# Two pieces at fixed places, four banks for the last shared products, two groups' sums on ScalarE and GpSimd, and a place for one turn

## The chip, the cores and the metric

The kernel runs on one core of one Trainium2 chip. The metric is the device time of an execution in microseconds (us). TensorE is called PE in the views, VectorE DVE, ScalarE ACT, GpSimd POOL and SyncE SP; SP and ACT issue most transfers, POOL issues those whose addresses come from a tensor.

## The reference

Input x has 32 sequences of 32 tokens of 256 features, all f32. Four residual steps follow each other; the last one is where most of the change lies.

```python
x = x + attn(cond(x, idx, weights))           # per-sequence mixing, layer norm, 16-head causal attention
x = x + ffn(lora_ffn(x, adapters))            # gated feed-forward with adapters (256 -> 1024 -> 256), then a second one
x = x + memory_attn(causal_attn(x, precision))  # 16 heads; then retrieval from four memory banks
x = x + moe(paged_attn(x, block_tables, kv_lens))

def moe(xt):                                   # 1024 tokens, 16 experts, two chosen for each token
    logits = xt @ Wr.T + bias
    probs = softmax(logits)
    val, idx = top_k(probs, 2)
    w = val / (sum(val) + 1e-9)
    y_e = (silu(xt @ Wg[e]) * (xt @ Wu[e])) @ Wd[e]          # for every expert e: 256 -> 128 -> 256
    routed = sum over the two chosen e of w * y_e
    shared = (silu(xt @ sWg) * (xt @ sWu)) @ sWd
    return routed + shared
```

## The kernel before

The tokens are worked in four quarters of 256 (`NQ = 4`) in the first two steps and in layer 1's first attention, and in eight groups of 128 (`NG = 8`) later. A framework records the program and orders the instructions of each engine; `behind(a, b)` fixes by hand that b stands behind a in its engine's queue. Each engine then runs its queue strictly in that order.

**The feed-forward with attention woven in.** `mha` is a generator with a step per `yield`. For each half j of a quarter it makes scores (L444, kb from L437), then the softmax on DVE and ACT: L456, L460, L461, the exponential L462, L464 to L466. It then turns the weights with four transposes into a bank (L470, "the turn"), copies them on ACT (`PT`, L472), multiplies with the values (L477, sixteen small products) and copies the outcome (`AV`, L484). `layer1(q, held=held)` runs this attention for quarter q, and the products that it puts into the dictionary `held` get a place inside the gated products of `feed_forward(q + 1, z, held)`. `gated` makes eight sums per half of its output in pairs (w_g, w_g, bl_g, or w_u, w_u, bl_u for each sum; L196); `sums_` lists their last matmuls in order. `STAND` says behind which of these sums what was held has to stand:

```python
for k, n in STAND.items():
    for x in held.get(k, ()):
        behind(sums_[n - 1], x)
```

ACT makes the feed-forward's tanh (L593), DVE its products (L594, L595). During the second of these rounds POOL fills a mask (`bad`, L818, L819).

**The expert pieces.** After the router each token has two rows, one for each chosen expert. Rows are ordered by expert into 16 blocks of 128 (`NB = 16`), and a block may hold rows of more than one expert, so there are at most `NP = 31` pieces, each one block with one expert. POOL gathers the blocks' rows (`xg`, L1476): nine gathers stand first in its queue, then a product of the shared expert (L1341), then the other gathers. TensorE turns each block (`xT`, L1566 and L1568). For piece j the expert `ex[j]` and the block `j - bx[j]` are read from registers: DVE copies the block into `xs` (L1577), TensorE multiplies it with the expert's gate and up weights out of `ew` (L1580), ACT and DVE make h (L1592, L1593), TensorE turns h (L1595), ACT copies it (`hT`, L1600), TensorE multiplies with the down weights (L1602), and DVE adds the rows that belong to the piece into `yall` (L1612). As soon as a block's last piece is in, POOL writes the block's rows to `ys_d` in DRAM in the tokens' order (L1617).

**The shared expert.** `shared_in` makes its hidden rows for 512 tokens (L1331, L1336, L1341 or L1343), `shared_out` multiplies for four groups of 128 tokens (L1350) and adds into `acc` (L1354). The first half's products stand at piece 2, the second half's after the last piece. They use the pool `y` of two banks.

**The end.** SP and ACT, in turn, read both rows of each token back from `ys_d`, one transfer for each group (`y2`, L1637). DVE multiplies each row by its weight and adds it to `acc` (L1641, two for each group), and SP (even groups) and ACT (odd groups) write the group out (L1644).

Of the kernel before, what the change touches and what calls it, by code (L numbers as in the profile page):

```python
# [18 lines left out]
F32 = mybir.dt.float32  # L19
I32 = mybir.dt.int32  # L20
AF = mybir.ActivationFunctionType
ALU = mybir.AluOpType
AX = mybir.AxisListType

P = 128
B, S, D = 32, 32, 256
# [23 lines left out]
NE = 16  # L50
# [3 lines left out]
NB = 2 * NT // P  # L54
NP = NB + NE - 1
# [73 lines left out]
def tile_layers(ctx: ExitStack, tc: tile.TileContext, i: dict, out: bass.AP):  # L129
    nc = tc.nc  # L130
    v, s, g_, te = nc.vector, nc.scalar, nc.gpsimd, nc.tensor
# [16 lines left out]
    ident = cpool.tile([P, P], F32, name="ident")  # L148
# [80 lines left out]
    turn = [cpool.tile([P, 2, NG, 32], F32, name=f"turn{j}") for j in range(2)]  # L229
# [3 lines left out]
    with (  # L233
# [169 lines left out]
        def mha(zq, w, q_out, k_out, v_out, ch=first_chain, idle=(), held=None):  # L403
# [27 lines left out]
            for j in range(QG):  # L431
                js = slice(j * P, (j + 1) * P)
                ps = ch.score()
                for m in range(2):

                    kb = ch.tile("kb", [P, 4, 8, 32])
                    v.tensor_tensor(  # L437
                        kb,
                        KT[:, m, js].rearrange("p (b k) -> p b k", b=4).unsqueeze(2).broadcast_to([P, 4, 8, 32]),
                        m8.unsqueeze(1).unsqueeze(3).broadcast_to([P, 4, 8, 32]),  # L440
                        ALU.mult,
                    )
                    for b4 in range(4):
                        mm_ = te.matmul(  # L444
                            ps[32 * b4 : 32 * b4 + 32, m * 256 : (m + 1) * 256],
                            lhsT=QT[:, m, j * P + 32 * b4 : j * P + 32 * b4 + 32],
                            rhs=kb[:, b4].rearrange("p h k -> p (h k)"),
                            start=True,
                            stop=True,
                        )  # L450
                        if held is not None:
                            held.setdefault(("scores", j, m), []).append(mm_)
                    if (j, m) in idle:
                        keep_busy(idle[j, m], ch.bank()[:, 0], w["q"][:, 0, :], mm_)
                sm = ch.tile("sm", [P, 16, 32])
                v.tensor_tensor(  # L456
                    sm, ps.rearrange("p (h k) -> p h k", k=32), C("causal").unsqueeze(1).broadcast_to([P, 16, 32]), ALU.add
                )
                mx = sp.tile([P, 16], F32, tag="mx", name="mx")
                v.tensor_reduce(mx, sm, AX.X, ALU.max)  # L460
                v.tensor_tensor(sm, sm, mx.unsqueeze(2).broadcast_to([P, 16, 32]), ALU.subtract)  # L461
                s.activation(sm, sm, AF.Exp)  # L462
                su = sp.tile([P, 16], F32, tag="su", name="su")
                v.tensor_reduce(su, sm, AX.X, ALU.add)  # L464
                v.reciprocal(su, su)
                weighted.append(v.tensor_tensor(sm, sm, su.unsqueeze(2).broadcast_to([P, 16, 32]), ALU.mult))  # L466
                yield
                pt = tr.tile([P, 4, P], F32, tag="tr", name="tr")
                for hg in range(4):
                    te.transpose(pt[:, hg], sm[:, 4 * hg : 4 * hg + 4, :].rearrange("p h k -> p (h k)"), ident)  # L470
                PT = sp.tile([P, 4, P], F32, tag="PT", name="PT")
                s.copy(PT, pt)  # L472
                yield
                av = tr.tile([P, 4, P], F32, tag="tr", name="tr")
                for b4 in range(4):
                    for hg in range(4):
                        te.matmul(  # L477
                            av[64 * (hg % 2) : 64 * (hg % 2) + 64, hg // 2, 32 * b4 : 32 * b4 + 32],
                            lhsT=vblk[:, j, b4, hg, :],
                            rhs=PT[:, hg, 32 * b4 : 32 * b4 + 32],  # L480
                            start=True,
                            stop=True,
                        )
                s.copy(AV[:, :, js], av[:, :2])  # L484
                yield
# [82 lines left out]

        STAND = {("scores", 1, 0): 4, ("scores", 1, 1): 5, "first": 14, "second": 15, "banks": 16}

        def lora(ps, q, name):

# [471 lines left out]
    with tc.tile_pool(name="w1", bufs=1, reuse_waits="tile") as wp:  # L1046
# [269 lines left out]
        with (  # L1316
# [26 lines left out]
                    eng.tensor_tensor(h, h, pair[1], ALU.mult)  # L1343
                return h

            def shared_out(n, h, pool, tag):
                for j in range(4):
                    g = 4 * n + j
                    ps = pool.tile([P, CH], F32, tag=tag, name=tag)
                    down = te.matmul(  # L1350
                        ps[:, :D], lhsT=h[:, j * P : (j + 1) * P], rhs=sd[:, 0, :], start=True, stop=True
                    )
                    behind(loaded[0][-1], down)
                    v.tensor_tensor(acc[:, g, :], acc[:, g, :], ps[:, :D], ALU.add)  # L1354
# [165 lines left out]
            with (  # L1520
# [39 lines left out]
                for j in range(NP):  # L1560
                    if j == 2:
                        shared_out(0, first_h, yp, "y")
                    if j < NB:
# [2 lines left out]
                            turned = te.transpose(pt[:, k * P : (k + 1) * P], xg[j][:, k * P : (k + 1) * P], ident)  # L1566
                            behind(gus[j - 2] if j > 1 else loaded[0][-1], turned)
                        v.tensor_copy(xT[:, j, :], pt[:, :D])  # L1568
                    w = ew[:, bass.ds(ex[j], 1), :].rearrange("p a n -> p (a n)")
                    at_b = nc.s_assert_within(  # L1570
                        j - bx[j],
                        max(0, j - NE + 1),
                        min(j, NB - 1),
                        skip_runtime_bounds_check_because="a piece's number is its block's and its expert's together",
                    )
                    x = sp.tile([P, 1, D], F32, tag="xs", name="xs")
                    v.tensor_copy(x, xT[:, bass.ds(at_b, 1), :])  # L1577
                    pg = gp.tile([P, CH], F32, tag="gu", name="gu")
                    for k in range(2):
                        mm_ = te.matmul(  # L1580
# [19 lines left out]
                    s.copy(hT, ph[:, :P])  # L1600
                    py = yp.tile([P, CH], F32, tag="y", name="y")
                    yd = te.matmul(py[:, :D], lhsT=hT, rhs=w[:, 2 * D :], start=True, stop=True)  # L1602
                    ys_.append((j, at_b, py))
                    if j == 1:
                        places()


                    while j >= 1 and ys_:
                        k, at_k, py = ys_.pop(0)
                        to_k = yall[:, bass.ds(at_k, 1), :].rearrange("p a n -> p (a n)")  # L1610
                        kept_.append(
                            v.scalar_tensor_tensor(to_k, py[:, :D], own[:, k : k + 1], to_k, ALU.mult, ALU.add)  # L1612
                        )
# [8 lines left out]
                            )  # L1622
                        )
                weigh()
                shared_out(1, shared_in(1, gp, "gu", v, yd), yp, "y")
                behind(picked[-1], *put)
                for j, a in enumerate(put):
                    for b in put[:j]:
# [9 lines left out]
                    y2s.append(y24[:, g % 4])  # L1638
                for g, y2 in enumerate(y2s):
                    for k in range(2):  # L1640
                        v.scalar_tensor_tensor(  # L1641
                            acc[:, g, :], y2[:, k, :], w12[:, k, g : g + 1], acc[:, g, :], ALU.mult, ALU.add
                        )
                    (nc.sync, s)[g % 2].dma_start(out[g * P : (g + 1) * P, :], acc[:, g, :])  # L1644
# [73 lines left out]
```

## Time and profile before

| What | us |
|---|---|
| median of 3 runs | 639.51 (638.82 to 641.37) |
| the profiled execution, its own time | 637.68 |
| its span | 635.9 |
| TensorE busy in the span | 576.7 |
| DVE busy | 383.4 |
| ACT busy | 179.3 |
| POOL busy | 184.0 |

The page gives busy times of each engine, the clock that was granted to TensorE in tenths in 40 slices of the span, and the chain of work that ended last, followed back from the end. Times in the other views are counted from the span's start. A line of the timeline has start, duration, engine, line of the kernel, operation, the tiles written and read with their shapes, the count, and in brackets how long the engine was idle before and what ended that. A line of the windows has a stretch, its length, then the busy time and count for PE, PE's weight loads, DVE, ACT and POOL, and last the granted clock, the DMA share and GB/s.

### The profile page before, as it was taken

To read this page: it belongs to the slowest core of one execution; us is meant where nothing else is said; L and a number is where in the kernel's file an instruction comes from. 1 tells how busy PE (TensorE), PEld (TensorE's weight loads), DVE (VectorE), ACT (ScalarE), POOL (GpSimd) and SP (SyncE) were. 2 spreads that over 40 slices of the span, in tenths; PEclk is the share of its full clock that TensorE was granted. 3 is DMA by queue.
4 is the path that set the end of the run, shared out by engine and by line. 5 is a ranking of instruction groups with operands and counts; after the bars stand their busy time and mean duration, and the time that the engine had idled before them with its cause. 6 is when DMAs were issued, how large, how long until landed. Compare 5 with 4: busy or idle time off the path is not lost.

```text
span 635.9 us, 9278 instructions
## 1 busy us (share of the span) xinstructions
PE 576.7 (91%) x3302; PEld 445.7 (70%) x3302; DVE 383.4 (60%) x893; ACT 179.3 (28%) x487; POOL 184.0 (29%) x268
## 2 busy tenths in 40 slices
PE   3889999999999999999999999997688898799992
PEld 1667878687778786788878886785566676466661
DVE  4847685965856939533382128546377775665655
ACT  1312232422312203122041103324365543312220
POOL 5014001434530048960000000005656402360350
PEclk9979999999999999999999999999599988989997
DMA  6963201645441000000000038004212100220126
GB/s 174 344 246 36 57 2 38 168 129 121 116 129 40 1 13 3 1 2 18 0 1 1 0 112 350 2 1 142 77 57 82 52 2 33 73 82 13 42 84 207
DMA packets 29165, 48.47 MB, mean 76 GB/s; under 512 B 7535, under 2 KB 21248, under 8 KB 28288
## 3 DMA queue, kind: packets, MB, share of 16 engines
q1 hardware_dynamic: 19405, 30.23, 14.0%
q0 software_dynamic: 5184, 15.38, 9.4%
q10 hardware_dynamic: 4531, 2.28, 1.3%
q8 instruction: 26, 0.43, 0.3%
q14 instruction: 19, 0.16, 0.1%
HBM read 36.84 MB, written 11.04 MB: 75 GB/s over the span
## 4 chain that ended last, share of the span: by engine, by line
PE 68%; DVE 18%; issue 4%; ACT 4%; DMA 3%; POOL 2%; another core or an unknown queue 1%; SPq 0%; DVEq 0%; ACTq 0%; POOLq 0%
PE ff L196 31%; PE mm L196 10%; PE gu L1580 4%; PE tr L477 3%; PE y L1602 2%; PE sc L1157 2%; DVE kb L437 2%; PE po L1191 2%; DVE vblk L427 2%; PE mm L939 2%; ACT sm L1172 2%; PE sc L444 1%; PE tr L470 1%; POOL xg L1476 1%
## 5 line engine op out<-in xcount | busy, mean ns | idle before, releaser
L1098 POOL DMA_INDIRECT kv<-rows_d,at x40 | 39.1, 977 | 173.2 <-DVE rsm L1012 152.3
L662 POOL COPY rr<-raw 88x256 f32<-88x256 f32 x64 | 30.3, 506 | 93.8 <-PE tr L525 47.4
L594 DVE SCALAR_TENSOR_TENSOR th<-th,ff 128x512 f32<-128x512 f32 x32 | 21.8, 682 | 38.4 <-ACT th L593 38.3
L437 DVE TENSOR_TENSOR kb<-KT,con 128x1024 f32<-128x1024 f32 x28 | 34.1, 1239 | 9.5 <-ACT KT L410 5.0
L1580 PE MATMUL gu<-ew,xs 128*128 x124 | 34.8, 401 | 2.1 <-DVE xs L1577 1.3
L593 ACT ACTIVATE th<-ff 128x512 f32<-128x512 f32 x32 | 19.1, 597 | 59.4 <-PE ff L196 56.0
L196 PE MATMUL ff<-x,w_g 128*128 128x256 f32 x128 | 35.6, 391 | 0.0
L196 PE MATMUL ff<-x,w_u 128*128 128x256 f32 x128 | 34.9, 386 | 0.0
L196 PE MATMUL ff<-y,f_w_gate 128*128 128x256 f32 x128 | 31.5, 381 | 0.0
L196 PE MATMUL ff<-y,f_w_up 128*128 128x256 f32 x128 | 31.1, 381 | 0.3 <-DVE th L594 0.3
L1172 ACT ACTIVATE sm<-sm,mx 128x160 f32<-128x160 f32 x64 | 26.7, 419 | 10.9 <-DVE mx L1170 7.5
L196 PE MATMUL ff<-h,d_Wd 128*128 128x256 f32 x128 | 29.8, 381 | 0.0
L196 PE MATMUL ff<-h,f_w_down 128*128 128x256 f32 x128 | 28.3, 379 | 0.0
L1580 PEld LDWEIGHTS gu<-ew,xs 128*128 128x128 f32 x124 | 22.9, 199 | 7.6 <-PE y L1602 3.2
L1191 PE MATMUL po<-PT,kv 128*128 128x256 f32 x64 | 19.8, 433 | 9.1 <-ACT PT L1188 7.7
L196 PEld LDWEIGHTS ff<-x,w_g 128*128 128x128 f32 x128 | 22.8, 189 | 7.4 <-issue 4.9
L1157 PE MATMUL sc<-KT,qz 128*128 128x160 f32 x128 | 25.7, 334 | 2.4 <-issue 1.5
L595 DVE SCALAR_TENSOR_TENSOR h<-th,ff 128x512 f32<-128x512 f32 x32 | 21.7, 680 | 9.4 <-PE ff L196 9.1
L196 PEld LDWEIGHTS ff<-x,w_u 128*128 128x128 f32 x128 | 23.5, 190 | 5.4 <-issue 2.2
L1166 DVE SCALAR_TENSOR_TENSOR sm<-bad,sc 128x320 f32<-128x320 bf16 x32 | 15.5, 485 | 19.5 <-PE sc L1157 7.1
L196 PEld LDWEIGHTS ff<-y,f_w_up 128*128 128x128 f32 x128 | 24.0, 190 | 4.0 <-DVE th L594 0.7
L196 PEld LDWEIGHTS ff<-y,f_w_gate 128*128 128x128 f32 x128 | 24.0, 190 | 4.0 <-issue 0.8
(418 smaller groups left out, 1301.6 us busy)
## 6 DMA issues: line engine op xcount, KB each, us to landing
ew<-in_L_ffn_W SPq DMA_DIRECT2D x1, 6144.0 KB
rows_d<-rr SPq DMA_DIRECT2D x32, 176.0 KB
x<-in_x SPq DMA_DIRECT2D x4, 256.0 KB
w_u<-in_L_cond_Wu SPq DMA_DIRECT2D x1, 1024.0 KB
w_g<-in_L_cond_Wg SPq DMA_DIRECT2D x1, 1024.0 KB
d_Wd<-in_L_cond_Wd SPq DMA_DIRECT2D x1, 1024.0 KB
f_w_gate<-in_L_ffn_w_gate SPq DMA_DIRECT2D x1, 1024.0 KB
f_w_up<-in_L_ffn_w_up SPq DMA_DIRECT2D x1, 1024.0 KB
```

The costliest lines, as they stand in the source:

```text
L196: mm_ = te.matmul(ps, lhsT=a, rhs=b, start=j == 0, stop=j == len(pairs) - 1)
L437: v.tensor_tensor(kb, KT[:, m, js].rearrange("p (b k) -> p b k", b=4).unsqueeze(2).broadcast_to([P, 4, 8, 32]), m8.unsqueeze(1).unsqueeze( ...
L477: te.matmul(av[64 * (hg % 2) : 64 * (hg % 2) + 64, hg // 2, 32 * b4 : 32 * b4 + 32], lhsT=vblk[:, j, b4, hg, :], rhs=PT[:, hg, 32 * b4 : 3 ...
L593: s.activation(t, pg, AF.Tanh, scale=0.5)
L594: v.scalar_tensor_tensor(flat(t), flat(t), 1.0, flat(pg), ALU.add, ALU.mult)
L595: v.scalar_tensor_tensor(flat(h[:, f : f + 2]), flat(t), 0.5, flat(pu), ALU.mult, ALU.mult)
L662: g_.tensor_copy(r[:, :, j].rearrange("p o g d -> p g o d"), raw[j].rearrange("p (g a o d) -> a p g o d", g=4, a=8, d=32)[a],)
L1098: got = g_.indirect_dma_start(out=kv[:, a, :], out_offset=None, in_=rows_d, in_offset=bass.IndirectOffsetOnAxis(ap=at[:, g, a : a + 1], ax ...
L1157: mm_ = te.matmul(ps[:, h, :], lhsT=q.qz[:, b, h].rearrange("p g t -> p (g t)"), rhs=q.KT[:, b, :], start=True, stop=True,)
L1172: exp_ = s.activation(sm[:, h], sm[:, h], AF.Exp, bias=mx[:, h : h + 1], accum_out=q.su[:, b, h : h + 1])
L1191: mm_ = te.matmul(q.po[:, b, : 2 * P], lhsT=q.kv[:, b, P:], rhs=PT[:, j, :], start=True, stop=False)
L1580: mm_ = te.matmul(pg[:, :D], lhsT=x[:, 0, k * P : (k + 1) * P], rhs=w[:, k * D : (k + 1) * D], start=k == 0, stop=k == 1,)
```

## The change

Four things change.

- The turn of the first half (j = 0) in `mha` is put into `held`, and `STAND` puts it behind the seventh sum of the feed-forward.
- The first piece takes expert 0 and block 0, the last piece expert 15 and block 15, as fixed addresses; `xs` and its copy are left out for these two, and TensorE reads `xT` itself.
- The second half's `shared_out` takes its third and fourth bank from the pool `xt`.
- For groups 2 and 4 ACT multiplies the rows by their weight in place, and POOL adds them to `acc`. The other six groups stay on DVE.

In the changed program's order of instructions the turn of j = 0 stands four matmuls later on TensorE in the second and the third of the three woven rounds, and in ACT's queue the copy `PT` of the first half then stands behind the exponential (L462) of the second half. DVE's queue keeps its order there. In ACT's queue of the end the four multiplications of groups 2 and 4 stand ahead of the four writes.

```diff
--- before.py
+++ after.py
@@ -467,7 +467,9 @@
                 yield
                 pt = tr.tile([P, 4, P], F32, tag="tr", name="tr")
                 for hg in range(4):
-                    te.transpose(pt[:, hg], sm[:, 4 * hg : 4 * hg + 4, :].rearrange("p h k -> p (h k)"), ident)
+                    t_ = te.transpose(pt[:, hg], sm[:, 4 * hg : 4 * hg + 4, :].rearrange("p h k -> p (h k)"), ident)
+                    if held is not None:
+                        held.setdefault(("turn", j), []).append(t_)
                 PT = sp.tile([P, 4, P], F32, tag="PT", name="PT")
                 s.copy(PT, pt)
                 yield
@@ -568,7 +570,7 @@
 
 
 
-        STAND = {("scores", 1, 0): 4, ("scores", 1, 1): 5, "first": 14, "second": 15, "banks": 16}
+        STAND = {("turn", 0): 7, ("scores", 1, 0): 4, ("scores", 1, 1): 5, "first": 14, "second": 15, "banks": 16}
 
         def lora(ps, q, name):
 
@@ -1343,9 +1345,11 @@
                     eng.tensor_tensor(h, h, pair[1], ALU.mult)
                 return h
 
-            def shared_out(n, h, pool, tag):
+            def shared_out(n, h, pool, tag, *more):
                 for j in range(4):
                     g = 4 * n + j
+                    if more and j == 2:
+                        pool, tag = more
                     ps = pool.tile([P, CH], F32, tag=tag, name=tag)
                     down = te.matmul(
                         ps[:, :D], lhsT=h[:, j * P : (j + 1) * P], rhs=sd[:, 0, :], start=True, stop=True
@@ -1566,15 +1570,22 @@
                             turned = te.transpose(pt[:, k * P : (k + 1) * P], xg[j][:, k * P : (k + 1) * P], ident)
                             behind(gus[j - 2] if j > 1 else loaded[0][-1], turned)
                         v.tensor_copy(xT[:, j, :], pt[:, :D])
-                    w = ew[:, bass.ds(ex[j], 1), :].rearrange("p a n -> p (a n)")
-                    at_b = nc.s_assert_within(
-                        j - bx[j],
-                        max(0, j - NE + 1),
-                        min(j, NB - 1),
-                        skip_runtime_bounds_check_because="a piece's number is its block's and its expert's together",
-                    )
-                    x = sp.tile([P, 1, D], F32, tag="xs", name="xs")
-                    v.tensor_copy(x, xT[:, bass.ds(at_b, 1), :])
+                    if 0 < j < NP - 1:
+                        w = ew[:, bass.ds(ex[j], 1), :].rearrange("p a n -> p (a n)")
+                        at_b = nc.s_assert_within(
+                            j - bx[j],
+                            max(0, j - NE + 1),
+                            min(j, NB - 1),
+                            skip_runtime_bounds_check_because="a piece's number is its block's and its expert's together",
+                        )
+                        x = sp.tile([P, 1, D], F32, tag="xs", name="xs")
+                        v.tensor_copy(x, xT[:, bass.ds(at_b, 1), :])
+                        at_ = bass.ds(at_b, 1)
+                    else:
+
+                        w, b = ew[:, 0 if j == 0 else NE - 1, :], 0 if j == 0 else NB - 1
+                        at_ = slice(b, b + 1)
+                        x = xT[:, at_, :]
                     pg = gp.tile([P, CH], F32, tag="gu", name="gu")
                     for k in range(2):
                         mm_ = te.matmul(
@@ -1600,14 +1611,14 @@
                     s.copy(hT, ph[:, :P])
                     py = yp.tile([P, CH], F32, tag="y", name="y")
                     yd = te.matmul(py[:, :D], lhsT=hT, rhs=w[:, 2 * D :], start=True, stop=True)
-                    ys_.append((j, at_b, py))
+                    ys_.append((j, at_, py))
                     if j == 1:
                         places()
 
 
                     while j >= 1 and ys_:
                         k, at_k, py = ys_.pop(0)
-                        to_k = yall[:, bass.ds(at_k, 1), :].rearrange("p a n -> p (a n)")
+                        to_k = yall[:, at_k, :].rearrange("p a n -> p (a n)")
                         kept_.append(
                             v.scalar_tensor_tensor(to_k, py[:, :D], own[:, k : k + 1], to_k, ALU.mult, ALU.add)
                         )
@@ -1622,7 +1633,7 @@
                             )
                         )
                 weigh()
-                shared_out(1, shared_in(1, gp, "gu", v, yd), yp, "y")
+                shared_out(1, shared_in(1, gp, "gu", v, yd), yp, "y", xp, "xt")
                 behind(picked[-1], *put)
                 for j, a in enumerate(put):
                     for b in put[:j]:
@@ -1638,6 +1649,10 @@
                     y2s.append(y24[:, g % 4])
                 for g, y2 in enumerate(y2s):
                     for k in range(2):
+                        if g in (2, 4):
+                            s.activation(y2[:, k, :], y2[:, k, :], AF.Copy, scale=w12[:, k, g : g + 1])
+                            g_.tensor_tensor(acc[:, g, :], acc[:, g, :], y2[:, k, :], ALU.add)
+                            continue
                         v.scalar_tensor_tensor(
                             acc[:, g, :], y2[:, k, :], w12[:, k, g : g + 1], acc[:, g, :], ALU.mult, ALU.add
                         )
```

## The prediction

> **What bounds the kernel now.** The page comes first: its engine line, its clock line, its chain.
>
> ```profile
> PE 576.7 (91%) x3302; PEld 445.7 (70%) x3302; DVE 383.4 (60%) x893; ACT 179.3 (28%) x487; POOL 184.0 (29%) x268
> ...
> PEclk9979999999999999999999999999599988989997
> PE 68%; DVE 18%; issue 4%; ACT 4%; DMA 3%; POOL 2%; another core or an unknown queue 1%; SPq 0%; DVEq 0%; ACTq 0%; POOLq 0%
> ```
>
> TensorE carries 68% of the chain that ended last, and its granted clock is full in most slices. A change off TensorE pays only where TensorE waits, so each edit is judged at its own place: the feed-forward stages with attention woven in (from 232 and from 314 us), the start of the expert pieces (549 to 562) and the end (from 622).
>
> The timeline at the moved turn, first at 248 us:
>
> ```profile
> 248.84 0.71 DVE L466 TENSOR_TENSOR sm<-sm,su 128x512 f32<-128x512 f32 x1
> ...
> 249.61 0.66 PE L470 MATMUL tr<-ident,sm 128*128 128x128 f32 x4 [1.04 <-DVE sm L466]
> ...
> 250.30 0.59 ACT L472 COPY PT<-tr 128x512 f32<-128x512 f32 x1 [2.97 <-PE tr L470]
> ...
> 250.76 0.86 POOL L819 TENSOR_TENSOR bad<-low,con 128x320 bf16<-128x320 f32 x1
> ...
> 250.91 1.26 DVE L461 TENSOR_TENSOR sm<-sm,mx 128x512 f32<-128x512 f32 x1
> ...
> 252.20 0.63 ACT L462 ACTIVATE sm<-sm 128x512 f32<-128x512 f32 x1 [0.82 <-DVE sm L461]
> ```
>
> TensorE stands still for 1.04 us before the turn. Note also which ACT instruction comes when: PT's copy at 250.30, the second half's exponential only at 252.20, because DVE's subtraction (L461) takes 1.26 us.
>
> The chain of waits at the pieces' start and the timeline at the end:
>
> ```profile
> 559.39 0.95 POOL xg L1476
> ...
> 560.36 1.28 POOL h L1341
> ...
> 561.68 0.70 PE y L1350 x2
> ...
> 622.78 6.39 DMA y<-ys_d
> ...
> 629.19 3.27 DVE acc L1641 x8
> ```
>
> ```profile
> 625.25 0.48 DVE L1641 SCALAR_TENSOR_TENSOR acc<-y,w,acc 128x256 f32<-128x256 f32 x1 [0.89 <-DMA y<-ys_d]
> 625.65 0.75 DVE L1354 TENSOR_TENSOR acc<-acc,y 128x256 f32<-128x256 f32 x2
> 626.32 2.46 DVE L1641 SCALAR_TENSOR_TENSOR acc<-y,w,acc 128x256 f32<-128x256 f32 x6
> 629.19 3.78 DVE L1641 SCALAR_TENSOR_TENSOR acc<-y,w,acc 128x256 f32<-128x256 f32 x9 [0.41 <-DMA y<-ys_d]
> ```
>
> At the start GpSimd's row of gathers and its product L1341 decide, not TensorE. At the end DVE adds 16 weighted rows at a pace of 2.46/6 = 0.41 us, in part behind the reads of ys_d.
>
> **Part 1: the turn behind the seventh sum.** In the changed order the four transposes L470 of j = 0 stand four matmuls (bl_g, w_u, w_u, bl_u) later, in the second and third rounds of layer 1 (the two places above). An f32 128x256 matmul is two records, and the chain has eight of them at 132.25 us in 1.73, so 0.43 us each. First place: the sums end at 248.56, four more end at 250.28, and the 1.04 us of idling is filled. But another thing moves too: ACT's copy PT (L472) of the first half now stands behind the second half's exponential in ACT's queue. DVE's order is unchanged, so that exponential still starts at 252.20 and ends at 252.83; PT's copy ends at 253.42 and the 16 products L477 start near 253.6. TensorE has only two matmuls between (end 251.8), so it idles 1.8 us. The products (1.06) and one matmul end at 255.1; the second turn stood at 255.01 before. So the filled gap comes back later: +0.1 us. A gain is excluded, since the second turn needs DVE's L466, which ended at 254.86. Second place: GpSimd is idle there, the exponential stands at 332.85, and TensorE had no such gap (turn at 330.82, next turn at 335.59). Now four matmuls to 332.4, turn and two matmuls to 333.8, PT's copy at 333.48 to 334.07, products from 334.25 to 335.3, one matmul: 335.75, so +0.2. Together I take +0.3 us, at full clock. Work behind the waiting products on TensorE is one matmul and the second turn, and behind PT on ACT the copies AV.
>
> A longer gap can cost clock. One trace row is a stretch before a half-clock stretch, the other the gap at 248.56:
>
> ```profile
> 246.63:250.04 3.41, 2.37 (x18) 1.27 (x17) 3.28 (x7) 0.63 (x1) 3.23 (x5) 1.00 0.00 0
> ...
> 526.52:529.93 3.41, 1.88 (x7) 0.96 (x7) 2.22 (x7) 1.22 (x5) 0.35 (x2) 1.00 0.00 0
> 529.93:533.34 3.41, 3.39 (x9) 2.14 (x8) 0.39 (x1) 0.96 (x2) 0.00 (x0) 0.50 0.00 0
> ```
>
> The first number after the stretch's length is TensorE's busy time. A stretch busy for 2.37 of 3.41 us (0.69) kept the clock; one busy for 1.88 (0.55) was followed by 3.41 us at half. The Trainium skill, "TensorE: Matmul & The Clock Gate", HAM oscillation, puts the rule as no idle gap above about 3.4 us; by it a gap of 1.8 costs nothing. By the trace it may: if it falls whole into one stretch (the page has them free-running), that is busy for 1.61 of 3.41 (0.47), and the next stretch does half its work: +1.7 us. The measurement decides against the rule; but the stretch may also split the gap, and where GpSimd's L819 misses DVE's L461 (0.69 us at 332 us), the gap is 1.2 and the share at least 0.65. I give it about 3 in 10 and keep it out of the sum.
>
> **Part 2: first and last piece at fixed places.** Two DVE copies xs (0.29 us) and the address work of six matmuls and two DVE sums go. At the start the first product L1580 can begin when xT is there (553.58 + 0.41, near 554.05) instead of 554.58: half a microsecond earlier. It is worth nothing: TensorE's next stop is at 561.68 for L1341 of GpSimd, which stands behind nine gathers (1.25 us apart from 549.30), none of which waits for TensorE. At the end the last pieces go in TensorE's own rhythm of 1.65 us, xs was copied at 611.44, 4 us ahead, and the last product waits for hT of ACT (617.47 to 617.74). So 0. Cover gone, the two sides would be -0.5 at the start, and a loss: see the rivals.
>
> **Part 3: four banks for the last shared products.** The third product stood until DVE freed a bank (0.5 us at 623.99), and the four ended at 625.12; now at 624.5. DVE's order keeps its first weighted sum, which waits for the rows of group 0 until 625.23, ahead of the third and fourth additions. So 0, covered by that transfer.
>
> **Part 4: groups 2 and 4 on ScalarE and GpSimd.** Four DVE sums go, 4 x 0.41 = 1.6 us. Added are four ACT scalings of 128x256 (nearest row L539, ACTIVATE 128x256: 0.47) and four GpSimd additions. L1341 takes 1.27 us for 512 columns and L788 0.317 for 64, so about 2.1 ns a column and 0.73 for 256. Behind them: on ACT the writes of groups 1, 3, 5, 7, now behind both groups' scalings; on SP the write of group 6 behind 2 and 4.
> If nothing collides: reads of group 2 land at 626.80 and of group 4 at 629.16; ACT scales group 4 by 630.1; GpSimd ends at 631.2; DVE ends groups 6 and 7 at 632.15 instead of 632.97. That is -0.8.
> The row that speaks against it is shown above: with GpSimd's L819 running from 250.76, DVE's L461, both of whose inputs lie in SBUF, took 1.26 us; the same line took 0.69 at 332.12 with GpSimd idle. The difference is what L819 still had to run. The Trainium skill, "SBUF — State Buffer", SBUF: two separate sides, has the rule: a DVE instruction with two SBUF inputs and a GpSimd one that reads SBUF share a port pair, and one fully blocks the other. DVE's L1641 and GpSimd's additions are exactly that pair. Serialised from 627.3, DVE has 9 sums left (about 3.6 us) and GpSimd 2.9: 633.8, so +0.8, and +1.0 if GpSimd is last, since SP then still issues two writes (0.34 us each). Rule and row weigh more than the free case; but over the trace L461 has a mean of 0.746, so most of its runs escaped, and two writes fewer run against the reads. I take +0.5, ends -0.8 and +1.0.
>
> **Sum.** +0.3 + 0 + 0 + 0.5 = +0.8 us. The profiled execution has a span of 635.9 and took 637.68 us, so 638.5 for it; it lies 1.83 below the median 639.51, so the median is forecast at 640.3.
>
> **The rivals.**
> A (0.50), the forecast: 640.3, with its own range 639 to 641.5.
> B (0.27), the clock closes: the gap of 1.8 us at 251.8 makes a stretch less than about 0.6 busy, and the next runs at half clock: +1.7, 642.0. The same at the pieces' start: the earlier first product fills the stretch 553.82 to 557.24 (busy 2.68 before), the clock opens one stretch earlier, TensorE ends its work near 559.5 and then waits for L1341 for 2 us; the stretch before 561 is then little more than half busy, and the shared products start at half clock, +1.2: 643.2 with both. For it: the row at 526 us. Against: the gap at 248 kept its clock. It decides where a stretch's busy share falls below 0.55 to 0.62.
> C (0.23), the end runs free: DVE and GpSimd do not block each other, or GpSimd works in DVE's waits; -0.8 and, with fewer writes against the reads, up to 0.7 more: 638.0 to 639.0. For it: DVE stands 0.4 us at 628.8 waiting for rows. Against: the 1.26 us row.
> That the four banks and the fixed pieces do nothing for the time is part of A, and each could be taken out alone without loss.
>
> **How the numbers follow.** What a measurement can tell from no change is about 0.5%, 3.2 us: 636.3 to 642.7. A lies within it; B passes 642.7 in about half of its cases, 0.13; C passes 636.3 only with lucky runs, and a general error of mine is left the rest: faster 0.05, same 0.82, slower 0.13. The range takes C's free end less half a microsecond for the runs' spread (638.8 to 641.4), 637.5, and B with both stretches, 643.2.
>
> **What would show it.** Right: in the timeline near 252 PT's copy after the exponential and a gap of 1.2 to 1.8 us before L477; no gap at 248.6; L1341 still ending near 561.6 with L1350 behind it; at the end L1641 or GpSimd's addition longer than 0.48 and 0.73 us where they overlap, last sum near 633.5. Wrong: the start of L1350 earlier than 561; sums of both engines side by side at their own speed and a last sum near 632; half-clock stretches between 250 and 260 or 560 and 568 (then B).

## The result and the profile after

The change makes the kernel slower by 0.8%: 643.66 us (641.28 to 648.90, 20 runs) against 639.35 us (637.21 to 643.92, 20 runs) of the kernel before, a ratio of 1.0079 with a 95% interval of 1.0059 to 1.0098, which is 3.8 to 6.3 us. The ratios here are taken over the fast runs of both kernels and are not quotients of the medians (643.66/639.35 is 1.0067); the two differ by up to 0.0012. The forecast was 640.3 with a range up to 643.2. So the time lies outside the range, by 0.5 us, and the case that came is the one that was given 0.13.

The two profiled executions stand further apart than the medians: 645.31 us after (1.65 above its median) and 637.68 before (1.67 below its median). Of the 7.6 us between the spans, 1.7 had arisen by 58.7 us (one DVE instruction, L437, starts there before and at 60.40 after), long before any changed instruction; the step is absent in other kernels that carry the same edits, so it is not read as an effect of the change. Another 1.5 came up by the first weighted sum of the end, with the stretches at half clock lying elsewhere in the two executions; the sums themselves took 0.2 less, and 4.6 came behind the last of them. All places are compared below against something near them.

The page of the changed kernel: its span, the busy time of the engines, the granted clock in 40 slices, the chain.

```profile
span 643.5 us, 9276 instructions
...
PE 575.5 (89%) x3302; PEld 443.9 (69%) x3302; DVE 382.9 (60%) x887; ACT 181.3 (28%) x491; POOL 188.8 (29%) x272
...
PEclk9979999999999999999999999999799998799996
...
PE 67%; DVE 16%; issue 4%; ACT 3%; DMA 3%; POOL 3%; another core or an unknown queue 1%; ACTq 0%; SPq 0%; DVEq 0%; POOLq 0%
```

TensorE's busy time is 1.2 us less and DVE's 0.5 less. ACT has 2.0 more, which is the four scalings, and GpSimd 4.8 more, of which the four additions are 3.2. TensorE, which bounds the kernel, has no more to do, so busy time does not say where the loss is. The chain does (start, duration, what):

```profile
626.21 7.02 DMA y<-ys_d
...
633.25 2.23 DVE acc L1656 x4
...
635.51 0.48 DVE acc L1656
```

It ends at 635.99, and the span only at 643.5: 7.5 us in which the chain has nothing. Before, the last sum ended at 632.97 and the span at 635.9: 2.9 us. The waits of SP's queue name an amount, first of the changed kernel and then of the kernel before (waiter, what it waited for, us in total, times, longest):

```profile
SPq L1729 <- PEq L1729: 5.3, 2, 4.6
...
SPq L1729 <- DMA out<-acc: 2.0, 3, 0.9
```

```profile
SPq L1714 <- DMA out<-acc: 2.0, 3, 0.9
...
SPq L1714 <- PEq L1714: 0.7, 2, 0.5
```

L1729, and L1714 before, is the end of the program. Waiting for the last writes costs 2.0 us in both. A second wait, of at most 0.5 us before, is 4.6 us long. The releaser in that line (TensorE's sequencer) is an inference; the instruction records of the trace, which hold the end-of-program instructions that the page does not count, show who is last. Engine, instruction, start, duration, end, in us:

```
before   GpSimd  DMA_INDIRECT (L1617, last put of ys_d)   619.29  0.97  620.26
before   GpSimd  DRAIN (end of program)                   619.05  9.29  628.34
before   Sync    DRAIN (end of program)                   635.09  0.01  635.10
after    GpSimd  TENSOR_TENSOR (L1654, last addition)     633.61  0.79  634.40
after    GpSimd  DRAIN (end of program)                   633.57  8.92  642.50
after    Sync    DRAIN (end of program)                   638.12  0.01  638.12
after    GpSimd  EVENT_SEMAPHORE (releases the others)    642.63  0.02  642.64
```

GpSimd's DRAIN ends 8.08 us after its last instruction before, and 8.10 after. Before, that instruction was the last put of weighted rows, and the 8.1 us passed while the rows were read back, added and written: covered, with 6.8 us to spare. After, GpSimd's last instruction is an addition that ends 14.1 us later, and SP, done at 638.12, waits 4.4 us for GpSimd.

The rest of the end, in the timeline (start, duration, engine, line, operation, count, and the idle time before it):

```profile
628.49 0.48 DVE L1656 SCALAR_TENSOR_TENSOR acc<-y,w,acc 128x256 f32<-128x256 f32 x1 [1.21 <-DMA y<-ys_d]
...
629.55 3.40 DVE L1656 SCALAR_TENSOR_TENSOR acc<-y,w,acc 128x256 f32<-128x256 f32 x6
633.25 2.74 DVE L1656 SCALAR_TENSOR_TENSOR acc<-y,w,acc 128x256 f32<-128x256 f32 x5 [0.30 <-DMA y<-ys_d]
```

```profile
630.55 1.72 POOL L1654 TENSOR_TENSOR acc<-acc,y 128x256 f32<-128x256 f32 x2 [7.38 <-ACT y L1653]
632.72 1.68 POOL L1654 TENSOR_TENSOR acc<-acc,y 128x256 f32<-128x256 f32 x2 [0.45 <-ACT y L1653]
```

Six sums in 3.40 us, where before six took 2.46. In the records, three of the twelve DVE sums take 0.94 or 0.95 us. Each of them starts 0.13 to 0.19 us into an addition of GpSimd and ends 0.28 us after it. The others take 0.47 to 0.56, among them the two that ran beside the third addition. So the blocking that the forecast priced is there, though not for every addition. But from the first weighted sum to the last it is 7.50 us (628.49 to 635.99) against 7.72 before (625.25 to 632.97): with four sums fewer and three of them twice as long, DVE ends 0.2 us sooner, and so does SP (9.63 us after the first sum against 9.85). That is less than profiles differ: in nine kernels with all sums on DVE it is 9.45 to 10.34.

The turn, on ACT and TensorE:

```profile
253.94 0.63 ACT L462 ACTIVATE sm<-sm 128x512 f32<-128x512 f32 x1 [2.73 <-DVE sm L461]
254.47 0.57 ACT L474 COPY PT<-tr 128x512 f32<-128x512 f32 x1
```

```profile
251.71 0.60 PE L470 MATMUL tr<-ident,sm 128*128 128x128 f32 x4
252.15 1.03 PE L196 MATMUL ff<-x,w_u 128*128 128x256 f32 x4
255.09 1.12 PE L479 MATMUL tr<-PT,vblk 128*64 128x32 f32 x32 [1.92 <-ACT PT L474]
```

The copy PT stands behind the exponential, the gap ahead of the turn is gone, and one of 1.92 us stands ahead of the products.

### The profile page after: what moved, and what is told of

Its sections match the earlier page's. It is cut to its first block, busy times and chain, and to the rows that moved or that the text cites. A ratio compares the mean times of both kernels' runs of the same rounds, so it can differ in the third digit from the quotient of the medians.

```text
span 643.5 us, 9276 instructions
## 1 busy us (share of the span) xinstructions
PE 575.5 (89%) x3302; PEld 443.9 (69%) x3302; DVE 382.9 (60%) x887; ACT 181.3 (28%) x491; POOL 188.8 (29%) x272
## 4 chain that ended last, share of the span: by engine, by line
PE 67%; DVE 16%; issue 4%; ACT 3%; DMA 3%; POOL 3%; another core or an unknown queue 1%; ACTq 0%; SPq 0%; DVEq 0%; POOLq 0%
PE ff L196 30%; PE mm L196 9%; PE gu L1591 4%; PE tr L479 3%; PE sc L1159 3%; PE y L1613 2%; DVE vblk L427 2%; PE sc L444 2%; DVE kb L437 2%; PE po L1193 2%; PE mm L941 2%; ACT sm L1174 1%; DVE AVT L1227 1%; PE tr L470 1%; POOL xg L1480 1%
## 5 line engine op out<-in xcount | busy, mean ns | idle before, releaser
L437 DVE TENSOR_TENSOR kb<-KT,con 128x1024 f32<-128x1024 f32 x28 | 33.8, 1229 | 10.9 <-ACT KT L410 5.0
L1591 PE MATMUL gu<-ew,xs 128*128 x116 | 31.7, 392 | 1.5 <-DVE xs L1582 1.5
L196 PEld LDWEIGHTS ff<-h,d_Wd 128*128 128x128 f32 x128 | 24.0, 190 | 3.9 <-issue 0.8
L196 PEld LDWEIGHTS ff<-h,f_w_down 128*128 128x128 f32 x128 | 24.3, 190 | 3.3
```

The source lines that it names most:

```text
L196: mm_ = te.matmul(ps, lhsT=a, rhs=b, start=j == 0, stop=j == len(pairs) - 1)
L437: v.tensor_tensor(kb, KT[:, m, js].rearrange("p (b k) -> p b k", b=4).unsqueeze(2).broadcast_to([P, 4, 8, 32]), m8.unsqueeze(1).unsqueeze( ...
L1591: mm_ = te.matmul(pg[:, :D], lhsT=x[:, 0, k * P : (k + 1) * P], rhs=w[:, k * D : (k + 1) * D], start=k == 0, stop=k == 1,)
```

## The experiments

Theory D (the drain): GpSimd's end of program takes 8.1 us from the end of its last instruction, whatever that is, and the program ends no sooner; the loss is what sticks out beyond the end of SP's work. Rival L (locking): the loss is DVE's sums and GpSimd's additions blocking each other, or the scalings and the writes behind them. Rival T: the other parts (turn, pieces, banks) lose time. Each group of four ran on one chip beside the kernel before, which had a median of 629.32 us in the first group, 637.38 in the second and 637.04 in the third; ratios are to it.

### Parts 1 to 3, and part 4 alone

The first kernel, e1_parts123, is the changed kernel without the four lines for groups 2 and 4. The second, e2_part4, is the kernel before with these four lines alone:

```diff
+                        if g in (2, 4):
+                            s.activation(y2[:, k, :], y2[:, k, :], AF.Copy, scale=w12[:, k, g : g + 1])
+                            g_.tensor_tensor(acc[:, g, :], acc[:, g, :], y2[:, k, :], ALU.add)
+                            continue
```

> The change without its fourth part: all sums of the end are back on DVE, the turn, the fixed pieces and the four banks stay. Theory D (GpSimd's own end of program takes 8.1 us from its last instruction, and the program waits for it): GpSimd's last instruction is again the write of rows at about 620 us, its end is covered, and the time is that of the kernel before within 1 us (ratio 0.999 to 1.002). Rival L (the loss is DVE and GpSimd blocking each other in the sums): also back to before, so this run does not part D from L. Rival T (the loss lies in parts 1 to 3: the turn, the clock, the wait of 1.6 us at 62 us that the changed kernel's trace shows): the time stays at about +4 us (ratio 1.006 to 1.008).

> The kernel before with the fourth part alone: groups 2 and 4 scaled on ACT and added on GpSimd. Theory D: GpSimd's last sum ends about 1.5 us before DVE's last, its end of program lasts 8.1 us more, and the program is 4 to 4.7 us longer (ratio 1.006 to 1.0075). Rival L: the same length only if DVE's last sum is later by 4 us; the changed kernel's trace has it 0.2 us earlier relative to the landing of group 0, so L gives 0 to +1. Rival T: 0 to +1.

Parts 1 to 3: 632.60 us, ratio 1.004 (1.0016 to 1.0064). That is above what theory D expected (0.999 to 1.002) and below T's 1.006 to 1.008. Part 4 alone: 634.22 us, ratio 1.0083 (1.0059 to 1.0108), as much as the whole change. In the profile of part 4 GpSimd's last addition ends at 624.58, its DRAIN at 632.68, SP is done at 628.31: 4.4 us again. The waits of SP's queue of that kernel:

```profile
SPq L1718 <- PEq L1718: 5.1, 2, 4.6
```

So part 4 alone makes a loss as large as the whole. The two losses together, 1.2%, are more than the whole change's 0.8%; the 0.4% of parts 1 to 3 is taken up again below.

### A one-column copy on GpSimd, and the same sums without GpSimd

The third kernel leaves every sum on DVE and adds to the kernel before one GpSimd instruction that nobody waits for, a copy of one column of group 4's rows; the result is not used.

```diff
+                    if g == 4:
+                        g_.tensor_copy(gs_[:, :1], y2[:, 0, :1])
```

The fourth does part 4 with the additions on DVE (the edit is against the second kernel):

```diff
-                            g_.tensor_tensor(acc[:, g, :], acc[:, g, :], y2[:, k, :], ALU.add)
+                            v.tensor_tensor(acc[:, g, :], acc[:, g, :], y2[:, k, :], ALU.add)
```

> The kernel before with one more GpSimd instruction, a copy of one column behind the landing of group 4's rows (629.2 us in the trace of before); all sums stay on DVE. Theory D: GpSimd's end of program runs from 629.4 to 637.5 instead of to 628.3, while SP ends at 635.1, so about +2.4 us (ratio 1.003 to 1.005). Rival L: one column blocks nothing, so 0 (0.999 to 1.001).

> The kernel before with groups 2 and 4 scaled on ACT as in the change, but added on DVE, no sum on GpSimd. Theory D: no GpSimd instruction at the end, so 0 to +0.5 us (DVE has as many instructions as before and may wait for ACT's scaling once; ACT's writes stand behind the scalings). A rival that puts the loss on ACT's queue (writes of groups 1 and 3 held back behind the scalings) gives most of the +4. On the blocking: if DVE's sums of 0.95 us in the changed kernel come from GpSimd, all of DVE's sums here take 0.48; if they come from ACT's scaling or from the transfers, some take 0.9 here too.

The copy takes 0.18 us and ends at 619.61; the DRAIN ends at 627.71, 8.10 us later, and SP was done at 625.31. The waits:

```profile
SPq L1716 <- PEq L1716: 3.1, 2, 2.6
```

It costs 1.0054 (1.0028 to 1.0080), where the 2.4 us that stick out are 1.0038. DVE's sums are untouched, so L cannot make this loss. With the additions on DVE the ratio is 1.0003 (0.9984 to 1.0023): the scalings on ACT and the writes behind them cost nothing that can be measured, and they gain nothing either. It also settles what made sums of 0.94 us. DVE's weighted sums, first in the changed kernel and then in this one (count, shortest, median and longest in ns, first and last start, shapes):

```profile
L1656 DVE SCALAR_TENSOR_TENSOR acc<-y,w,acc x12: 473/482/951, 628.5 to 635.5; 128x256 f32<-128x256 f32 x12
```

```profile
L1645 DVE SCALAR_TENSOR_TENSOR acc<-y,w,acc x12: 478/480/485, 618.0 to 625.6; 128x256 f32<-128x256 f32 x12
```

The scalings and the transfers are there in both; without additions on GpSimd no sum is long.

### The copy early and last, group 0 alone, the turn alone

The same copy at group 0, and of `acc` of group 7 after the last sum; part 4 for group 0 in place of 2 and 4 (the edit is against the second kernel); the turn's new place alone (the lines that put the transposes into `held` are as in the change and are left out here):

```diff
+                    if g == 0:
+                        g_.tensor_copy(gs_[:, :1], y2[:, 0, :1])
```

```diff
+                    if g == 7:
+                        g_.tensor_copy(gs_[:, :1], acc[:, 7, :1])
```

```diff
-                        if g in (2, 4):
+                        if g == 0:
```

```diff
-        STAND = {("scores", 1, 0): 4, ("scores", 1, 1): 5, "first": 14, "second": 15, "banks": 16}
+        STAND = {("turn", 0): 7, ("scores", 1, 0): 4, ("scores", 1, 1): 5, "first": 14, "second": 15, "banks": 16}
```

> The kernel before with one GpSimd copy of one column behind the landing of group 0's rows (625.2 us in the trace of before). Theory D: GpSimd's end of program then runs from 625.4 to 633.5, still ahead of SP's end at 635.1, so 0 (ratio 0.999 to 1.001). A rival in which any GpSimd instruction at the end costs as such gives the same +2.4 as a late one.

> The kernel before with one GpSimd copy of one column behind DVE's very last sum (633.0 us in the trace of before). Theory D: GpSimd's end of program runs from 633.2 to 641.3 against SP's end at 635.1: +6.2 us (ratio 1.008 to 1.011), more than the whole change lost, though nothing of the work is changed. Rival (a late GpSimd instruction costs a fixed amount): the same as with the copy behind group 4.

> The fourth part done for group 0 alone, the first to land (625.2 us): two scalings on ACT and two additions on GpSimd, which then ends near 627.4. Theory D: its end of program ends at 635.5, 0.4 us after SP's, and DVE is rid of two sums (0.8 us) less what the additions block (up to 0.9): between -0.5 and +0.6 us (ratio 0.999 to 1.001). If each sum on GpSimd cost by blocking or by its queue alone, half of the loss of the whole part would stay: +2.

> The first part alone: the turn behind the seventh sum. My prediction's step gives +0.3 us at full clock (gap of 1.04 at 248 us replaced by one of 1.2 to 1.9 at 252), +1.7 more where a stretch of half clock follows. Rival: the turn carries a good part of the loss, +2 or more, with half-clock stretches behind it. In the trace: gap before L470 gone, gap before L477 near 252 us in its place, the second turn at the same time within 0.3 us.

The same instruction costs nothing at group 0 (638.15 us, 1.0014, 0.9992 to 1.0036) and 1.0110 (1.0070 to 1.0150; 645.04 us, six runs) after the last sum. The page's waits of the latter:

```profile
SPq L1716 <- PEq L1716: 6.9, 2, 6.4
```

Part 4 for group 0 alone is at 638.23 us, 1.0005 (0.9980 to 1.0031), although one of its DVE sums was blocked and took 0.82 us. The turn alone is at 638.38 us, 1.0009 (0.9985 to 1.0033). All kernels side by side, with the end of GpSimd's last instruction, of its DRAIN, and of SP's work, in us from the start of each profile:

| kernel | GpSimd's last ends | DRAIN ends | between | SP done | sticks out | as a ratio | measured ratio |
|---|---|---|---|---|---|---|---|
| before | 620.26 | 628.34 | 8.08 | 635.10 | 0 | | |
| copy at group 0 | 622.42 | 630.51 | 8.09 | 632.40 | 0 | 1.0000 | 1.0014 |
| group 0 on GpSimd | 624.28 | 632.38 | 8.10 | 631.99 | 0.4 | 1.0006 | 1.0005 |
| copy at group 4 | 619.61 | 627.71 | 8.10 | 625.31 | 2.4 | 1.0038 | 1.0054 |
| part 4 alone | 624.58 | 632.68 | 8.10 | 628.31 | 4.4 | 1.0070 | 1.0083 |
| whole change | 634.40 | 642.50 | 8.10 | 638.12 | 4.4 | 1.0069 | 1.0079 |
| copy after the last sum | 634.88 | 642.98 | 8.10 | 636.77 | 6.2 | 1.0097 | 1.0110 |

"As a ratio" is what sticks out over the median of before in that group. It lies inside the measured interval in every row. In five of the six rows the measured ratio is higher by 0.0010 to 0.0016, and for part 4 alone and the two copies of group 0 and group 4 it is a little above what was expected; the intervals cannot tell this from nothing. Theory D holds with its size: the same one-column copy costs nothing, 0.5% or 1.1% as its own end comes later. L is there in the sums' durations and is not the loss.

### Pieces, banks, both, and the whole change without GpSimd

What is left is the 0.4% of parts 1 to 3. The first kernel has the fixed pieces alone, the second the four banks alone (of its edit the call is shown), the third both; the fourth is the whole change with one line changed, the additions of groups 2 and 4 on DVE, as above.

```diff
-                shared_out(1, shared_in(1, gp, "gu", v, yd), yp, "y")
+                shared_out(1, shared_in(1, gp, "gu", v, yd), yp, "y", xp, "xt")
```

```diff
-                            g_.tensor_tensor(acc[:, g, :], acc[:, g, :], y2[:, k, :], ALU.add)
+                            v.tensor_tensor(acc[:, g, :], acc[:, g, :], y2[:, k, :], ALU.add)
```

> Part 2 alone: the kernel before with the first and the last piece at fixed places; nothing else changed. D (GpSimd's end of program is the whole loss): no new GpSimd work at the end, ratio 1.000, within 0.998 to 1.002. Prediction's own step: 0, since the earlier first product waits for L1341 of GpSimd, which should end at the same time as before. Clock theory K (TensorE's earlier first product lowers the busy share of the stretches around 557 to 561 us, so that half-clock stretches appear there): +1.2 us, ratio 1.002, mean granted clock lower by 0.003. G (the order of gathers and of the products' waits loses 0.5 us or more between 560 and 578 us): ratio 1.001 to 1.004 at an unchanged clock, seen as an offset of the DVE instructions that arises there.

> Part 3 alone: the kernel before with the third and fourth of the last shared products in the turns' two banks; nothing else changed. Every theory: the four products end about 0.6 us earlier, the additions stand behind the first weighted sum that waits for the rows of group 0, so 0, ratio within 0.998 to 1.002. If parts 1 to 3 lose their 0.4% here, the ratio is 1.003 or more and the new place of the banks holds something up ahead of the end.

> Parts 2 and 3 together, without the turn's new place and without the sums on ScalarE and GpSimd. If the loss of parts 1 to 3 (ratio 1.004) comes from the turn with the pieces together (a clock stretch after the turn's gap), this stays at 1.000 to 1.002; if it comes from the pieces or the banks, 1.003 to 1.005.

> The whole change, only that the four additions of groups 2 and 4 run on DVE in place of GpSimd (ScalarE still scales). D: GpSimd's last instruction is again the last put of weighted rows, its end of program is over before SP is done, so the 4.4 us go; what is left is what parts 1 to 3 have, ratio 1.001 to 1.005. If the loss of the whole change came from ScalarE's scalings or the writes queued behind them on ACT, it stays at 1.008.

| kernel | us | ratio | 95% interval |
|---|---|---|---|
| fixed pieces | 637.34 | 1.0001 | 0.9971 to 1.0030 |
| four banks | 638.26 | 1.0011 | 0.9978 to 1.0044 |
| both | 637.77 | 1.0013 | 0.9984 to 1.0042 |
| whole change, additions on DVE | 636.68 | 1.0003 | 0.9978 to 1.0028 |

The last row decides: one line changed, the engine of four additions, and the 0.8% are gone. In its profile GpSimd's last instruction is the put of rows again (620.75), the DRAIN ends at 628.84 and SP is done at 635.98; the second wait of SP is back at its old size:

```profile
SPq L1729 <- PEq L1729: 0.7, 2, 0.5
```

In this kernel parts 1 to 3 are in place, and it does not confirm their 0.4%: 1.0003 lies just below the 1.001 to 1.005 that was expected. If the scalings on ACT cost nothing, as in part 4 with its additions on DVE, the two intervals overlap from 1.0016 to 1.0028, 1.0 to 1.8 us. Of the theories on the pieces, K (half-clock stretches near 557 to 561) fell: in the profile of the fixed pieces there is no half-clock stretch between 555.1 and 626.7. No version ran faster than the kernel before by more than its interval, so there is none to recommend.

One thing that differs between profiles can be seen, the clock after the turn's gap. The four profiles that have the turn's new place differ there (stretch, length, busy time of PE, PEld, DVE, ACT, POOL with counts, granted clock, DMA). Parts 1 to 3:

```profile
252.04:255.45 3.41, 1.49 (x14) 1.04 (x14) 3.24 (x5) 1.10 (x2) 3.15 (x5) 1.00 0.01 2
255.45:258.87 3.42, 3.42 (x39) 3.07 (x37) 1.88 (x3) 0.37 (x1) 3.24 (x4) 0.50 0.02 5
```

The whole change with the additions on DVE:

```profile
250.85:254.26 3.41, 1.49 (x30) 1.06 (x28) 3.21 (x6) 1.10 (x2) 3.15 (x4) 1.00 0.01 2
254.26:257.67 3.41, 3.41 (x23) 2.88 (x20) 1.46 (x2) 0.96 (x2) 3.13 (x5) 0.50 0.02 5
```

The whole change:

```profile
250.60:254.01 3.41, 2.58 (x14) 1.92 (x13) 3.34 (x5) 0.67 (x2) 3.23 (x4) 1.00 0.00 0
254.01:257.43 3.42, 2.34 (x39) 2.00 (x40) 2.97 (x5) 1.42 (x4) 3.24 (x5) 1.00 0.01 2
```

The gap is 1.92 us in each. Where it falls whole into one stretch, TensorE is busy for 1.49 of 3.41 us (0.44), and the next stretch runs at half clock; where two stretches share it (0.76 and 0.68), the clock stays. The turn alone is like the whole change. It costs 1.5 us where it happens: from the start of the waiting products to the second half's products it is 4.56 and 4.60 us in the first two kernels against 3.08 in the third. Two profiles of four show it.

That this makes the difference between the 1.004 and the 1.0003 is not shown, and it is not likely: the profiles of both these kernels have the stretch at half clock, and the turn alone has the same mean granted clock over its runs as the kernel before (0.9709 against 0.9711). The two ratios do differ by the clock of their runs, whatever sets it: parts 1 to 3 had 0.9745 against 0.9796 of before, the whole change with the additions on DVE 0.9743 against 0.9709. A straight line through the runs of before gives 0.32 us for each 0.001 of clock in the first group and 0.35 in the third. Above that line the two kernels lie by 2.3 us (1.6 to 3.0) and 2.2 us (1.5 to 2.9). So a loss of about 2 us from parts 1 to 3 is likely. With the 4.4 us of the drain that makes 6.4, at the upper edge of what the whole change lost (3.8 to 6.3). This is a fit over runs and not an experiment, and which of the parts has it stays open.

## Why the prediction was wrong

**Part 4, the step that failed.** The sum took the end of the last sum and of SP's last writes for the end of the program: "DVE ends groups 6 and 7 at 632.15 instead of 632.97. That is -0.8", and "+1.0 if GpSimd is last, since SP then still issues two writes". It had no term for what GpSimd does after its last instruction. That term is 8.1 us, and the trace of before had it: a DRAIN that ended at 628.34, under a cover that lasted until 635.10. The forecast named the cover of every part that it set to nothing and overlooked this one; the views that it read do not count such instructions. With it, the forecast's own free case would have given nearly the right answer: GpSimd's last addition at 631.2, plus 8.1 is 639.3, less 635.1 is +4.2; with +0.3 for the turn the median comes to 644.0. Measured is 643.66. The terms that the forecast did weigh there (four sums fewer, blocked sums, later writes) were put at +0.5. In the profile of the whole change they come to -0.2 and in that of part 4 alone to +0.4 (SP done 10.21 us after the first sum against 9.85), both inside the spread of 9.45 to 10.34.

**The blocking.** Right as a mechanism and near in size. The Trainium skill, "SBUF — State Buffer", SBUF: two separate sides, says that one fully blocks the other, and the trace agrees: 0.94 us for a sum of 0.48 that starts within an addition of 0.78 to 0.86, and 0.48 for all where DVE does the additions. It hit three sums of twelve, not all that were possible; whether four sums fewer outweighed it is inside the spread. Rival C, in which nothing blocks, fell with it. Its lower end was also summed wrongly: 639.5 + 0.3 - 0.8 - 0.7 is 638.3, not 638.0. And the row of L461 was read too exactly: it took 0.57 us more, where L819 still had 0.71 to run.

**Part 1.** Right, by its own signs: no gap ahead of the turn, PT's copy behind the exponential, a gap of 1.92 us where 1.8 was worked out, and 1.0009 (0.9985 to 1.0033) for the turn alone against +0.3 us. Where the clock stays full, in the profiles of the turn alone and of the whole change, DVE's instructions at 300 us are no later against the kernel before than at 247 us, ahead of the turn. If parts 1 to 3 lose the 2 us that the fit gives, +0.3 was too little for them; by itself that would have left the time inside the range.

**Rival B, the clock.** The first half of it is real: a gap of 1.92 us can be followed by 3.41 us at half clock. The price was put at 1.7 us and the chance at 3 in 10; it was 1.5, in two profiles of four. The Trainium skill, "TensorE: Matmul & The Clock Gate", HAM oscillation, with its idle gap of about 3.4 us, would have called such a gap free. The measurement decides, and it agrees with the busy share that the forecast took from the trace. But B is not why the range failed: in the profile of the changed kernel the clock stays full there, and part 4 alone, which leaves the turn in its place, has the loss. The second half of B did not come in that profile: the stretch at half clock around the pieces' start was 6.83 us long before and after, and the shared products ran at full clock.

**Part 2.** The cover held. GpSimd's gathers and its product still decide, first in the kernel before and then in the changed one:

```profile
560.36 1.27 POOL L1341 TENSOR_TENSOR h<-h,up 128x512 f32<-128x512 f32 x1
561.68 0.70 PE L1350 MATMUL y<-sh_d,h 128*128 128x256 f32 x2 [0.62 <-POOL h L1341]
```

```profile
562.47 1.27 POOL L1343 TENSOR_TENSOR h<-h,up 128x512 f32<-128x512 f32 x1
563.79 0.70 PE L1354 MATMUL y<-sh_d,h 128*128 128x256 f32 x2 [1.23 <-POOL h L1343]
```

TensorE waits 1.23 us for it instead of 0.62. The profiles leave room for a small loss behind that place (theory G of the fixed pieces' run). Against the kernel before, DVE's instructions move by -0.1 to +0.5 us between 553.9 and 577.9 us in the five kernels with the fixed pieces, and by -0.2 to 0.0 in the seven without them. A shift that differs so between profiles is not a measured loss, and the timing (1.0001, 0.9971 to 1.0030) allows none as well as one of this size.

**Part 3.** Right: 1.0011 (0.9978 to 1.0044) against 0.

**The chances.** Faster and same had 0.87 together because each case ended within DVE's and SP's last microsecond. A case on the other side, that the engine which is given new work late ends last for a reason of its own, was not among the rivals.

## What to carry to other kernels

Ask of each engine when its last instruction ends, and not only of the engine that ends last. In these kernels the program could not end before 8.1 us after GpSimd's last instruction. Even a one-column copy, ended less than that ahead of the others' end, cost what was missing, and the same copy at the start of the tail was free. When the span of a profile ends many microseconds after the chain's last piece, compare that rest with the one before (7.5 us against 2.9 here) and look for who holds the end. A gap on TensorE is not to be judged by its length alone: one of 1.92 us cost another 1.5 where it fell into one stretch of 3.41 us.

## What the runs showed of the hardware

The time from GpSimd's last instruction to the end of its DRAIN is 8.08 to 8.10 us in all fourteen kernels profiled, and the same for an indirect transfer (0.97 us), an addition of 256 columns (0.79) and a copy of one column (0.18). The DRAINs of DVE and ACT at the same place take 0.53 and 0.15 us in the changed kernel and end 0.05 and 0.19 us after the engine's last instruction. What GpSimd does in that time the traces do not show.

The share of a stretch in which TensorE is busy goes with the clock of the next one. Cut into the stretches of 3.41 us on which the clock is granted, the fourteen profiles have 39 at full clock that were busy for less than 0.45, and the next ran at half clock in all of them. Of 407 that were busy for 0.60 to 0.90 it did so in none, and between 0.45 and 0.60 in 26 of 46. The share is not the whole of it, for six stretches near 510 us were busy throughout and half clock followed all the same. In the kernel before:

```profile
509.46:512.87 3.41, 3.41 (x29) 2.95 (x31) 1.54 (x4) 1.51 (x6) 0.23 (x1) 1.00 0.00 0
512.87:516.28 3.41, 3.41 (x20) 2.71 (x12) 2.17 (x5) 1.47 (x6) 0.24 (x1) 0.50 0.00 0
```

Most matmuls of that first stretch write 16 columns; whether this is the reason is not shown.
